# Weight preparation moved into the first stage of a four-layer graph kernel, and its first two stages put into one ordered region

## The chip, the cores and the metric

One core of a Trainium2 chip runs the whole program. Its engines work through their own instruction streams and wait for one another on semaphores: TensorE (PE, with its weight loads shown apart as PEld), VectorE (DVE), ScalarE (ACT), GpSimd (POOL) and SyncE (SP), which here does nothing but issue DMAs. The metric is device time in microseconds (us), the median of three runs: 2710.17 us before the change (2709.83 to 2714.95).

## The reference, cut to what matters

The input is 128 graphs of 128 nodes with 128 features each, and a 0/1 adjacency matrix per graph. Four attention layers follow one another, each as `x = x + layer(relu(layernorm(x)), adj, weights)`. Only layer 0 bears on the change:

```python
def layer0(x, A):                                  # x: 128 graphs x 128 nodes x 128
    D = abs(x[:, :, None, :] - x[:, None, :, :])   # every pair of nodes
    h = einsum('bijc,oc->bijo', D, W1) + b1        # 64 outputs for a pair
    m, v = mean and variance of h over all graphs and all pairs
    h = leaky((h - m) / sqrt(v + EPS) * g1 + be1)
    s = einsum('bijo,uo->biju', h, W2)[..., 0] + b2[0]
    A = softmax(where(A > 0, s, NEG))
    y = einsum('bij,bjc->bic', A, x) @ Wg.T + bg
    y = leaky(batchnorm(y)) ; return concat([x, y]) @ Wt.T + bt
```

The mean and the variance `m`, `v` are taken over all pairs of all graphs, so no score of any graph can be finished before every pair has been seen. The weights of layers 1 to 3 (`L1_...`, `L2_...`, `L3_...`) are only brought into another form at the start of the program: transposed, multiplied with one another, summed.

## The kernel before, in words

The program has four parts, one after the other in time.

**Preparation** (lines 185 to 369). Small weights are loaded as columns by DMAs issued on POOL (`column`, L201 and L203, and L220 to L223). Larger ones are loaded by SP (`raw`, L261) and ACT (L277 to L344). Then PE, ACT and DVE transpose and combine them: `transposed` (L263, L264), the columns `fw` of layer 1 (L276 to L288), `w2g` (L316 to L319), `of_f1`, `of_f2` and `parts_m` (L293 to L308), `aT` and `aq` (L330 to L340), `vpw` (L346), `pb_row` and `pb_bc` (L351 to L360), `q_avg` (L364 to L369). Their scratch tiles lie in the pool `wload`, which is closed before the first stage opens its own pools in the same memory.

**First stage**, `statistics` (L490). It sees every pair of nodes and collects mean and variance. `nodes(g)` handles 4 graphs: it loads `xg` (L525), takes means and variances of the rows on DVE (L530, L531), `rs` on ACT (L535, L536), `xn` on POOL (L539, L540), stores it to DRAM, transposes on PE (L545), takes the ReLU `he` on ACT (L548), stores that to DRAM too, and works out three bf16 parts `us` of `pu` (L557 to L566). `block(b, q)` takes 32 rows of a graph against the 64 (or 63) nodes after each: the differences `d` on DVE (L605) or on POOL (L610), their absolute value on ACT (L614) unless a maximum was taken, the product with `w1T` on PE into a PSUM tile `ph` (L631), and the sums of it on DVE (`bn_stats`, L643) or on ACT (L637). There are 512 blocks. Blocks which take the maximum need `both` (L512 to L516) and `w1T2` (L518), which are made from the identity and from `w1T`. Nine `d` and three `ph` are in rotation. After the last block a chain of some thirty small instructions (L657 to L700) makes `h_sc` and `h_bi` from the collected sums.

**Second stage**, `edge_attention` (L702). It begins with its constants: `off` and `at` on POOL (L716, L721), `in_half`, `in_other`, `not_own`, `upto`, `down_d`, `ones`, `least`, `room` and others on DVE (L728 to L758), and `own_d`, which needs `h_bi` (L768 to L776). Then `group(g)` handles 4 graphs: three loads on SP (L793 to L795), `adjb` on POOL (L802), `half` and `other` on POOL (L810, L811), `rank` and `key_row` on PE (L815 to L817), `more`, `ranks`, `pos` and `row` on DVE (L820 to L832), `in_row` on PE (L836), the selection matrices `inc` on DVE (L843). Beside it `parts` splits `xn` into three bf16 tiles (ACT L867, DVE L869, POOL L875 and L876), `values` makes `pz` and `zg`, `check` makes `pc` (L892 to L898), `bases` makes `base` and `edge` (ACT L908, POOL L910 and L912). `graph` then takes, for each graph, the differences of the nodes that are joined by an edge (`diff`, PE L923), their absolute value (ACT L930), the product with `w1T` (PE L934), `z` with `h_sc` and `h_bi` (ACT L937), and the scores; `attention` takes the softmax. Three groups can hold input tiles at a time (`B_IN`).

**Third stage.** The remaining layers, four graphs at a time. Which of two versions runs is read from the tile `types` at L2386, and the engines all stop there for it.

**What sets the order.** Inside each of the first two stages the order of instructions on PE, ACT, DVE and POOL is written out by a planner, `in_order` (L64). Each piece of work is a generator which says `yield engine, planned us, tiles taken, tiles freed` ahead of the instructions it emits. The planner keeps a time for each engine at which it is free and always takes the piece which can begin first; between pieces that can begin at the same time it takes the older. `yield "after", event` holds a piece until an event, `yield "wait", us` adds to its planned time. The planned times decide only the order; on the chip an engine goes through that order and waits where an input is late. Outside the two `manual_schedule` regions (L652 and L1091), the framework orders the instructions by itself. The two regions and what lies between them run one after the other: the pools of the second stage reuse the memory of the first.

## Time and profile before

One execution was profiled. Its own device time is 2713.54 us; its span from the first to the last instruction is 2711.7 us, so 1.8 us lie around the span. The profiled run is 3.4 us above the median of the three runs. The granted TensorE clock is 0.966 of full speed on average.

| stretch of the profiled execution | from | to |
|---|---|---|
| preparation, up to the first `xg` load | 0 | 21.5 us |
| first `nodes`, up to the first difference block | 21.5 | 35.6 us |
| difference blocks, to the last one of POOL | 35.6 | 1079.9 us |
| last block on PE | | 1090.0 us |
| second stage, up to its first full `diff` | 1090.2 | 1115.9 us |
| second stage, to the read of `types` | | 1772.4 us |
| third stage | 1772.4 | 2711.7 us |

| engine | busy in the span | share |
|---|---|---|
| PE | 2497.3 us | 92% |
| DVE | 2416.1 us | 89% |
| ACT | 2161.6 us | 80% |
| POOL | 1644.8 us | 61% |

How to read it: busy shares over the whole span mix stages with different limits, so the stages are looked at one by one. In a view of stretches each row gives, behind the stretch and its length, the busy time of every engine (and its instructions), then the granted clock of TensorE, the share of the DMA engines that was busy, and GB/s. In a timeline each row is a start time, a duration, the engine, the line of the program, the operation, what is written and read, and in brackets how long the engine had stood idle and what released it. `SPq` is an issue of a DMA on SyncE.

### The profile page before, as it was taken

To read this page: it belongs to the slowest core of one execution; us is meant where nothing else is said; L and a number is where in the kernel's file an instruction comes from. 1 tells how busy PE (TensorE), PEld (TensorE's weight loads), DVE (VectorE), ACT (ScalarE), POOL (GpSimd) and SP (SyncE) were. 2 spreads that over 40 slices of the span, in tenths; PEclk is the share of its full clock that TensorE was granted. 3 is DMA by queue.
4 is the path that set the end of the run, shared out by engine and by line. 5 is a ranking of instruction groups with operands and counts; after the bars stand their busy time and mean duration, and the time that the engine had idled before them with its cause. 6 is when DMAs were issued, how large, how long until landed. Compare 5 with 4: busy or idle time off the path is not lost. (4 is left out here: it accounts for less than half of the span.)

```text
span 2711.7 us, 51703 instructions
## 1 busy us (share of the span) xinstructions
PE 2497.3 (92%) x19597; PEld 1559.2 (57%) x19597; DVE 2416.1 (89%) x4660; ACT 2161.6 (80%) x3531; POOL 1644.8 (61%) x943
## 2 busy tenths in 40 slices
PE   6999999999999999799999999968988888898888
PEld 3334333434333333577777777756766767667666
DVE  6999999999999998788988888778988888889886
ACT  4999999999999999466566666568787877787885
POOL 7999999999999999635435343022333333333234
PEclk8999999999999999899999999979999999999999
DMA  2000000000000000523222231040211111111001
GB/s 69 16 27 30 24 24 28 24 24 24 24 24 24 24 20 9 161 74 100 81 85 86 78 100 42 17 137 6 62 29 54 36 44 44 41 42 33 9 2 33
DMA packets 134257, 122.62 MB, mean 45 GB/s; under 512 B 9504, under 2 KB 100960, under 8 KB 134000
## 3 DMA queue, kind: packets, MB, share of 16 engines
q1 hardware_dynamic: 131360, 117.83, 14.1%
q8 instruction: 158, 2.59, 0.4%
q10 hardware_dynamic: 2032, 1.31, 0.2%
q14 instruction: 99, 0.81, 0.1%
q0 software_dynamic: 608, 0.07, 0.0%
HBM read 73.05 MB, written 46.14 MB: 44 GB/s over the span
## 5 line engine op out<-in xcount | busy, mean ns | idle before, releaser
L610 POOL TENSOR_TENSOR d<-he 128x2016 f32<-128x2016 f32 (+1 forms) x272 | 959.8, 3559 | 15.0 <-DVE six L643 7.8
L631 PE MATMUL ph<-d,w1T 128*64 128x504 f32 (+1 forms) x4096 | 910.0, 594 | 22.9 <-DVE six L643 13.2
L614 ACT ACTIVATE d<-d 128x2048 f32<-128x2048 f32 (+1 forms) x448 | 832.2, 1888 | 18.1 <-POOL d L610 12.4
L631 PEld LDWEIGHTS ph<-d,w1T 128*64 128x64 f32 x4096 | 320.2, 136 | 545.0 <-issue 459.9
L605 DVE SCALAR_TENSOR_TENSOR d<-pt,he 128x2048 f32<-128x2048 f32 x240 | 541.4, 2269 | 0.7 <-PE ph L631 0.7
L643 DVE BATCH_NORM_STATS2 six<-ph 128x6 f32<-128x512 f32 (+1 forms) x704 | 435.8, 676 | 13.4 <-PE ph L631 12.0
L1568 POOL TENSOR_TENSOR xn<-xo,mv 128x512 f32<-128x512 f32 x64 | 73.9, 1155 | 324.8 <-DVE mv L1561 257.5
L975 PE MATMUL pl<-its,it 128*128 128x128 f32 x1280 | 168.2, 280 | 1.5 <-DVE its L968 1.2
L875 POOL CAST h<-xn 128x512 bf16<-128x512 f32 x32 | 21.5, 672 | 243.5 <-DVE xn L869 229.4
L637 ACT ACTIVATE ph<-ph 128x1008 f32<-128x1008 f32 x160 | 159.7, 998 | 9.8 <-PE ph L631 8.8
L975 PEld LDWEIGHTS pl<-its,it 128*128 128x128 f32 x1280 | 154.4, 193 | 15.0 <-DVE its L968 6.5
L1671 DVE SCALAR_TENSOR_TENSOR p<-z,mask 128x1024 f32<-128x1024 f32 x124 | 147.7, 1210 | 8.3 <-ACT z L1669 8.0
L1569 POOL TENSOR_TENSOR xn<-xn,rs 128x512 f32<-128x512 f32 x96 | 111.1, 1158 | 49.6 <-ACT rs L1565 37.9
L937 ACT ACTIVATE z<-ph,h_bi,h_sc 128x320 f32<-128x320 f32 x128 | 78.5, 617 | 74.5 <-PE ph L934 73.8
L923 PE MATMUL diff<-inc,h 128*128 128x320 bf16 x768 | 130.0, 306 | 2.9 <-DVE inc L843 2.5
L1669 ACT ACTIVATE z<-z 128x1024 f32<-128x1024 f32 x128 | 129.0, 1008 | 4.0
L930 ACT ACTIVATE d<-diff 128x640 f32<-128x640 f32 x128 | 89.8, 702 | 52.9 <-PE diff L923 51.7
L843 DVE SCALAR_TENSOR_TENSOR inc<-in_row,row 128x4 bf16<-128x4 f32 (+12 forms) x512 | 125.5, 315 | 1.2 <-PE in_row L836 1.2
L965 ACT CAST it<-pi 128x640 f32<-128x640 bf16 x128 | 87.0, 689 | 47.3 <-PE pi L962 46.1
L1568 POOL TENSOR_TENSOR xn<-x,mv 128x512 f32<-128x512 f32 x32 | 36.5, 1139 | 138.3 <-DVE mv L1561 65.9
L968 DVE TENSOR_TENSOR its<-pi,s 128x640 f32<-128x640 bf16 x128 | 102.9, 810 | 15.0 <-ACT it L965 14.1
L1700 PE MATMUL va<-p,vals 128*32 128x128 f32 x2048 | 107.8, 283 | 8.0 <-DVE vals L1685 7.8
(349 smaller groups left out, 5349.8 us busy)
## 6 DMA issues: line engine op xcount, KB each, us to landing
ht<-h SPq DMA_DIRECT2D x64, 256.0 KB, 2.8
xg<-in_x SPq DMA_DIRECT2D x32, 256.0 KB, 2.7
n<-ln_xn SPq DMA_DIRECT2D x32, 256.0 KB, 2.4
h<-he SPq DMA_DIRECT2D x32, 256.0 KB, 2.6
adj<-in_adj SPq DMA_DIRECT2D x32, 256.0 KB, 3.1
xn<-n SPq DMA_DIRECT2D x32, 256.0 KB, 2.7
xb<-in_x SPq DMA_DIRECT2D x32, 256.0 KB, 3.3
xb<-xb SPq DMA_DIRECT2D x32, 256.0 KB, 2.0
```

The costliest lines, as they stand in the source:

```text
L605: nc.vector.scalar_tensor_tensor(dv, own, 0.0, later, ALU.max, ALU.max if is_larger else ALU.subtract)
L610: nc.gpsimd.tensor_tensor(dv, later, own, ALU.subtract)
L614: nc.scalar.activation(d[:, 0 : 4 * n], d[:, 0 : 4 * n], AF.Abs, accum_out=sums[:, g, k : k + 1] if on_act else None,)
L631: nc.tensor.matmul(ph[64 * a : 64 * a + 64, t, 0:n], wt, x_, start=part == 0, stop=not is_larger or part == 3,)
L637: nc.scalar.activation(ph[:, :, 0:n], ph[:, :, 0:n], AF.Square, accum_out=squares[:, g, k : k + 1])
L643: nc.vector.bn_stats(six[g][:, 2 * by_bn.index((i, q)) + t, :], ph[:, t, 0:n])
L843: nc.vector.scalar_tensor_tensor(inc[:, :, e : e + n], in_row[:, :, 0:n], float(k + 1), row[:, :, 0:n], ALU.is_equal, ALU.subtract,)
L923: nc.tensor.matmul(diff[:, a, 0 : SLOT_N // 2], h[:, i, :], inc[:, a * SLOT_N // 2 : (a + 1) * SLOT_N // 2], start=m == 0, stop=m == 2,)
L975: nc.tensor.matmul(made["pl"][:, i, :], it[:, k, :], its[:, k, :], start=k == 0, stop=k == 4)
L1569: nc.gpsimd.tensor_tensor(xn, xn, bcast(rs, 2, P), ALU.mult)
L1669: nc.scalar.activation(z, z, AF.Exp, scale=1.0 - SLOPE)
L1671: nc.vector.scalar_tensor_tensor(p, z, 1.0, bcast(mask[:, i, :], 1, NH), ALU.max, ALU.mult)
```

## The change

The diff does the following.

- `x` for the first eight graphs (`raw_x`) is loaded at once, on SP, as the first and third DMA of the program; the weights come after it. The columns that POOL loaded are now loaded by SP; five square weights are loaded by ACT, after the activation table, which is now loaded at the start; all other weights are loaded by SP. The scratch tiles lie in pools on the other side of the memory, apart from those of the stages.
- The computing part of the preparation becomes generators of the planner (`first_weight`, `own_and_later`, `attention_weights`, `square_weights`), run under `others` as second piece of the first stage. So do the constants of the second stage (`edge_constants`). `both` is added up on POOL instead of DVE. The PSUM tiles of the preparation are taken from the stage's `ph`. One more piece may be under way (`A_UNDER_WAY + 1`).
- Both stages lie in one `manual_schedule` region. The planner returns the times at which each engine and PSUM bank becomes free, and the second stage is planned from those. The tiles that a group needs ahead of `inc` lie in the pool `mid`, outside the first stage's memory; pieces that use reused memory wait for the event `begun`, pieces that need the mean and variance wait for `stats`. The chain of small instructions that makes `h_sc` and `h_bi` is a generator (`total`) in a fixed order, with two of its products on PE joined into one.

```diff
-def in_order(makers, most, room, kept):
+def in_order(makers, most, room, kept, begun=None):
...
-    free_at = dict.fromkeys(AFTER, 0.0)
-    slots = {kind: [0.0] * n for kind, n in room.items()}
-    chains, events = [], {}
+    free_at = dict.fromkeys(AFTER, 0.0) if begun is None else dict(begun)
+    slots = {kind: [0.0] * n if isinstance(n, int) else list(n) for kind, n in room.items()}
+    chains, events = [], {"begun": max(free_at.values())}
...
+    nc.scalar.preload_act_table_set("natural_log_exp_and_others")
...
+    raw_x = [wl.tile([P, GB, P], F32, tag=f"x{g}", name=f"x{g}") for g in range(2)]
+    nc.sync.dma_start(raw_x[0], x_t[:, 0:GB, :])
...
+    raw("w1", w["L0_gnn_W1"], nc.sync)
+    nc.sync.dma_start(raw_x[1], x_t[:, GB : 2 * GB, :])
+    raw("wg", w["L0_gnn_Wg"], nc.scalar)
...
-        nc.gpsimd.dma_start(t[0:n], src)
+        nc.sync.dma_start(t[0:n], src)
...
+    def attention_weights():
+        yield "wait", 20.0
+        yield DVE, 2.9, "", ""
         nc.vector.memset(fw, 0.0)
...
+    def square_weights(psum2):
+        yield "wait", 8.0
+        yield PE, 1.3, "ph", ""
+        pt = psum2("w_ps").rearrange("p a (b c) -> p (a b) c", c=P)
+        for k, name in enumerate(("wg", "wt0", "wt1", "kw", "pw")):
+            nc.tensor.transpose(pt[:, k, :], raws[name], ident)
+        yield ACT, 0.9, "", "ph"
+        nc.scalar.copy(w_T, pt[:, 0:4, :])
...
+        yield "wait", 12.0
+        yield PE, 1.7, "ph", ""
+        pv = psum2("vw_ps")
...
+    def edge_constants():
+        yield "wait", 30.0
+        yield POOL, 0.6, "", ""
+        nc.gpsimd.iota(
+            off, pattern=[[1, P]], base=0, channel_multiplier=-1,
+            allow_small_or_imprecise_dtypes=True,
+        )
...
-            nc.vector.tensor_tensor(
-                both.rearrange("p (i j) -> p i j", j=64),
-                shifted(ident[:, 1:65], QR), bcast(ident[:, 0:QR], 2, 64), ALU.add,
-            )
...
+            def own_and_later():
+                yield POOL, 3.9, "", ""
+                nc.gpsimd.tensor_tensor(
+                    both.rearrange("p (i j) -> p i j", j=64),
+                    shifted(ident[:, 1:65], QR), bcast(ident[:, 0:QR], 2, 64), ALU.add,
+                )
+                yield DVE, 0.68, "", ""
+                nc.vector.tensor_scalar(both, both, -1.0, None, ALU.mult)
+                yield "done", "both"
...
+            def first_weight():
+                yield "wait", 4.0
+                yield PE, 0.3, "ph", ""
...
+                if g < len(raw_x):
+                    xg = raw_x[g]
+                    yield "wait", 4.0 + 1.2 * g
+                else:
...
+            makers = [partial(nodes, 0), others]
...
+            begun = dict.fromkeys(AFTER, 1.0) | {POOL: 1.5, ACT: 5.0, DMA: 22.0}
+            free_at, slots = in_order(
+                makers, A_UNDER_WAY + 1, {"d": A_D, "ph": 3} | two, A_KEPT, begun
+            )
+        wl_pool.__exit__(None, None, None)
...
+        def total(psum, done):
+            yield "after", "begun"
+            yield DVE, 1.0, "", ""
...
+            yield PE, 0.4, "", ""
+            nc.tensor.matmul(pm[:, 1:4], q_avg, bn_m, start=True, stop=True)
+            yield DVE, 3.6, "", "p"
...
+            yield "done", "stats"
...
-            off = one_of("off", [P, P])
-            nc.gpsimd.iota(
...
-                xn, ht = tile_f("xn", B_IN), tile_f("ht", B_IN)
+                xn, ht = tile_i("xn", F32), tile_i("ht", F32)
...
+                yield "after", "begun"
                 for a, b in ((0, 2), (2, 4), (4, len(SLOTS))):
                     work = sum(0.1 + 0.00104 * GB * n for n in SLOTS[a:b])
                     yield DVE, work, "", "p" if b == len(SLOTS) else ""
+                    if a == 0:
+                        inc = b3p.tile([P, GB, SLOT_N], BF16, tag="inc", name="inc")
...
+                yield "after", "stats"
                 yield ACT, 0.53, "", "p"
                 z = made["z"][:, i, :]
                 nc.scalar.activation(z, ph, AF.Identity, bias=h_bi, scale=h_sc)
...
-            with tc.manual_schedule(engines=ORDERED):
-                in_order(
...
+            in_order(
+                makers, B_GROUPS, {"p": banks[0:6], "q": banks[6:7], "in": B_IN, "w": B_W, "d": 3, "it": 3, "ge": 1, "eT": 2, "yt": 2, "xb": 2}, {"p": 1}, free_at
+            )
...
-    statistics()
-    edge_attention()
+    with tc.manual_schedule(engines=ORDERED):
+        edge_attention(*statistics())
```

## The prediction

> **What bounds the kernel now.** I read the page's slices first (POOL, DVE and PE are full in the first stage, PE and DVE in the second), then the timeline at the start and at the border between the stages, then busy time by stretch. The chain of waits stops at the read of `types`, so it says nothing of these stages. From the timeline of the start:
>
> ```profile
> 0.74 0.59 SPq L261 DMA_DIRECT2D raw<-in_L_gnn_W  x1
> ...
> 20.70 0.76 PE L359 MATMUL ppb<-pb_row,ones_row 1*128 1x128 f32 x2 [0.71 <-DVE pb_row L357]
> 21.49 6.49 SPq L525 DMA_DIRECT2D xg<-in_x  x3
> ...
> 24.25 0.29 DVE L530 BATCH_NORM_STATS2 ln_s<-xg 128x6 f32<-128x128 f32 x1
> ...
> 35.58 17.60 POOL L610 TENSOR_TENSOR d<-he 128x2016 f32<-128x2016 f32 x5
> ```
>
> `x` is asked for only when the last product of the preparation is out of the scratch memory; its first use follows 2.76 us later, the first difference block 11.3 us after that. From the timeline of the border, the last rows of the first stage and the first of the second:
>
> ```profile
> 1089.48 0.60 PE L631 MATMUL ph<-d,w1T 128*64 128x504 f32 x2
> ...
> 1090.17 0.39 SPq L793 DMA_DIRECT2D adj<-in_adj  x1
> ...
> 1093.35 0.61 POOL L802 CAST adjb<-adj 128x512 bf16<-128x512 int32 x1 [13.46 <-DMA adj<-in_adj]
> ...
> 1106.20 0.39 PE L815 MATMUL rank<-upto,other 128*128 128x128 bf16 x4
> ...
> 1115.94 1.49 PE L923 MATMUL diff<-inc,h 128*128 128x320 bf16 x5 [2.47 <-DVE inc L843]
> ```
>
> POOL stands idle from 1079.9, 13.46 us long; the loads start when PE has finished; the first stream of edge differences comes 25.9 us after PE's end (1115.94 - 1090.08). Busy time by stretch (columns: PE, PEld, DVE, ACT, POOL, granted clock, DMA share, GB/s):
>
> ```profile
> 0.00:21.86 21.86, 8.77 (x32) 4.70 (x32) 7.67 (x40) 3.87 (x10) 11.48 (x27) 0.95 0.32 80
> 35.50:45.00 9.50, 6.58 (x26) 2.37 (x28) 8.05 (x7) 6.13 (x6) 9.50 (x4) 0.57 0.25 81
> 45.00:1079.90 1034.90, 1015.10 (x5156) 406.93 (x5154) 1020.00 (x1259) 1013.97 (x1062) 1017.30 (x358) 1.00 0.07 23
> 1090.00:1150.00 60.00, 42.73 (x319) 31.15 (x318) 47.49 (x173) 27.70 (x54) 45.90 (x44) 0.83 0.60 182
> 1150.00:1772.00 622.00, 593.41 (x5171) 461.21 (x5169) 520.89 (x1348) 382.24 (x813) 239.31 (x216) 0.98 0.23 73
> ```
>
> The first stage is full on four engines at once: 98.6% DVE, 98.3% POOL, 98.1% PE, 98.0% ACT. The second is PE's: 95.4%. So the time lies in three places: before the blocks, the blocks, the border.
>
> **Start.** The load of `x` goes from 21.49 to about 0.74, SP's first slot (the row of the W1 load). It shares the DMA engines with weights; of the old loads at the start the slowest took 4.7 us to land, the lone `xg` loads in 2.7. I take 3.0, so the first statistics stand at 3.7. The table load (1.28 us, now ahead of ACT's loads) ends long before ACT's first use. From first statistics to first block 11.3 us stay: 15.0 instead of 35.6, **20.6 us gained**. What could be late inside those 11.3: the sum of `both` moves from DVE (2.29 us) to POOL. The trace has this pair of engines on nearly one shape: differences take 3.56 us on POOL, 2.27 on DVE, factor 1.57, so 3.6 us, from 1.6 to about 5.2, just before POOL is wanted at 5.3. The Trainium skill, "GPSIMD Engine Reference" (4.1 Engine selection), puts two-input work at about twice VectorE's time: 4.6 us, end 6.2, and the start later by 0.9. I keep the row.
>
> SP now issues some 26 further loads, 0.4 to 0.6 us each: the last at about 15, landed by 20; the generators are planned for 21 and later. Behind them on SP is the first store of `xn`; a third `nodes` needs its tile, but is planned after DMA's 22.0.
>
> A second weighing, the clock. "TensorE: Matmul & The Clock Gate" (Part 1, "What's actually happening") says that half rate is the default and is lifted by about 3.4 us of sustained work; by it the new first `nodes` runs cold, like the old one, whose eight `pu` products took 1.76 us against 1.1 warm (33.1 us over 30 groups in the blocks). The trace grants 1.00 at the start and falls to 0.50 only after PE's pause behind 21.5. By the row, one set of `nodes` saves 0.45 in transposes (1.11 against 0.66) and 0.66 in `pu`, 1.1 us. I leave it out and use it for the range.
>
> **Blocks.** Moved in: DVE 7.67 - 0.3 (memsets that stay first) = 7.3 us of preparation, and 3.4 of constants (busy 3.45 of 3.6 us from 1095.6), together 10.7; PE 8.8; ACT 3.87 - 1.28 = 2.6; POOL two iotas of 0.24. The old cover was an otherwise idle machine; now they lie in a stage whose DVE has 14.9 us free in 1034.9. The waits of DVE there are 8.8 us on PE's `ph`, which are not slots that work may fill at will: PE waits as long for DVE (13.2 in the page's row), in turn, with three `ph`. Lower end: all of it fits, 0. Upper: DVE's 10.7 and PE's 8.8 never overlap, 19.5. Nearest row: at the ramp (35.5 to 45) DVE has 1.45 us idle. 10.7 - 1.4 = **9.3 us lost**. PE's part is taken beside it, since PE waited for DVE anyway.
>
> **Border.** The planner starts the second stage from the times at which each engine is free, so its work on PE still comes behind PE's last block, but POOL's behind POOL's last at 1079.9 and the loads earlier still. For three groups POOL has `adjb` 0.61 and `other`, `half` 1.15 each: 8.7 us, inside the 10 us in which PE and ACT finish. Then `rank` follows PE's last block instead of coming 16.1 us later (1106.20 - 1090.08). From `rank` to the stream of `diff` it took 9.7 us; in that stretch DVE must now also do the chain of small sums, which the old order laid largely beside the last blocks (1081.9 to 1095.4): about 28 instructions of 0.15 us, 4 us. So 25.9 becomes 13.7: **12.2 us gained**. Next late is DVE (sums, `row`, `inc` in one queue), then `z`, which waits for `h_bi`; behind it on ACT are the other groups' copies.
>
> Ends: none of it, and 4 us lost, if the loads or tiles come no earlier and the sums stand in one row; or all that PE lost there, 17.3 us idle between 1090 and 1150 and a clock of 0.83 over 42.7 busy us, some 7: 24 us. If PE, fed with `pz` and `rank` at once, keeps its clock, part of the 7 comes back. 12 is the middle of these, and the one that the rows give.
>
> The second stage after it is kept at 622 us of PE-bound work, the third unchanged.
>
> **Sum.** -20.6 + 9.3 - 12.2 = -23.5: span 2711.7 to 2688.2, the profiled execution 2713.54 to 2690.0. The median of the runs was 2710.17, 3.4 below it, so I forecast **2686.7**.
>
> **Rivals.**
> 1. *Border gain fails*: `inc`, `base` and `zg` wait for `begun` anyhow, and DVE is the queue for both chains. For it: from 1091.3 to 1119.6 DVE is busy 20.7 of 28.3. Against it: POOL, busy 21.6 there, begins 13 us earlier. -20.6 + 9.3 + 0 = -11.3: 2698.9.
> 2. *Work vanishes in gaps*: DVE's 14.9 free us take the weights, PE stays warm. For it: four engines that wait for each other by turns leave slack on all. Against: no wait on DVE exceeds 1.3 us. -20.6 + 2 - 18 = -36.6: 2673.6.
> 3. *The added load costs twice*: 19.5 in the blocks and nothing at the border: -1.1, 2709, no change. For it: the weights hold one of three `ph` across engines. Against: four holdings only.
> 4. *Slower*: the second stage's order is planned anew from uneven starting times and banks, and PE's share there falls. Its place is 1150 to 1772, where PE is busy 593.4 us. It decides when it eats 23.5 + 5.4 us: 622 + 29 = 651, a share of 91.2% instead of 95.4. At 90% the stage takes 659, +37: 2724. For it: the planner's durations are estimates. Against: the same pieces, the same number of tiles in rotation.
> That the change does not do what it says (the loads stay behind a wait on SP) is the first rival at the border; at the start nothing stands ahead of `x`.
>
> **How the numbers follow.** Forecast with its own spread (2679 to 2694): 0.62. Rival 1: 0.14. Rival 2: 0.12. Rival 3: 0.06. Rival 4: 0.06. A measurement of this kernel can tell about 0.2%, 5.4 us, from no change. Faster: 0.62 + 0.14 + 0.12 = 0.88; within: 0.06; slower: 0.06. The range takes in rival 1 and most of rival 2: 2672 to 2702.
>
> **What would show it.** First statistics near 3.7 and first `d` near 15; the last POOL block 11 us earlier than 1079.9; POOL not idle after it, `adjb` at once; `diff` within 15 us of PE's last block; the read of `types` near 1749. Wrong if DVE shows waits on weight loads in the first 25 us, if the blocks stretch by far more or less than 9 us, if SP still issues the `adj` loads only after the last block, or if PE's share in the second stage moves by over one point.

## The result, and the profile after

The changed kernel takes 2702.51 us (2699.1 to 2704.5 in seven runs) against 2711.97 us (2709.62 to 2721.8) for the kernel before in the same comparison: ratio 0.996, 95% interval 0.9945 to 0.9974. It is faster, as forecast, but by 9.5 us (0.35%) and not by 23.5; 2702.5 lies just outside the forecast's range of 2672 to 2702. The profiled execution took 2704.5 us with a span of 2702.7, 9.0 below the 2711.7 of before, and I work with that pair.

In the changed kernel the stage's lines moved: `d` is L706 on POOL and L701 on DVE, `ph` L727, the block statistics L739, `nodes` L618 to L662, `rank` L887, `inc` L917, `diff` L1001. From the timeline of the changed kernel, the start and then the border between the stages:

```profile
3.98 0.29 DVE L623 BATCH_NORM_STATS2 ln_s<-x 128x6 f32<-128x128 f32 x1 [2.91 <-DMA x<-in_x]
...
12.71 3.55 POOL L706 TENSOR_TENSOR d<-he 128x2016 f32<-128x2016 f32 x1
...
24.41 0.73 SPq L865 DMA_DIRECT2D adj<-in_adj  x1
...
1087.33 15.67 PE L727 MATMUL ph<-d,w1T 128*64 128x512 f32 x72
1090.63 1.74 POOL L874 CAST adjb<-adj 128x512 bf16<-128x512 int32 x3
...
1104.26 0.38 PE L887 MATMUL rank<-upto,other 128*128 128x128 bf16 x4 [1.26 <-ACT ph L733]
...
1124.67 1.49 PE L1001 MATMUL diff<-inc,h 128*128 128x320 bf16 x5 [2.40 <-DVE inc L917]
```

The first block starts at 12.7 instead of 35.6. The graph loads are issued at 24.4, a thousand microseconds ahead of their use; POOL goes on with `adjb` as soon as its last block ends at 1090.6, and `rank` follows PE's last block (1103.0) by 1.3 us. These moves did what they say. But the last block is late, not early, and the full stream of `diff` comes 21.7 us after it. Busy time by stretch of the changed kernel (columns as before: PE, PEld, DVE, ACT, POOL, granted clock, DMA share, GB/s):

```profile
12.50:46.00 33.50, 23.00 (x90) 9.30 (x89) 31.14 (x28) 14.32 (x17) 32.71 (x12) 0.80 0.53 151
46.00:76.00 30.00, 24.13 (x100) 8.89 (x100) 27.18 (x84) 20.04 (x21) 0.77 (x2) 0.89 0.00 1
76.00:1090.60 1014.60, 990.75 (x5016) 396.84 (x5016) 998.17 (x1232) 986.30 (x1034) 996.78 (x353) 0.99 0.08 24
1103.00:1125.00 22.00, 9.20 (x70) 6.79 (x71) 17.07 (x64) 8.06 (x17) 9.60 (x10) 0.73 0.51 155
1125.00:1763.00 638.00, 616.78 (x5405) 482.76 (x5413) 557.20 (x1415) 399.71 (x849) 260.98 (x240) 0.98 0.25 77
```

The hole is in the first two rows. In the first 34 us of the blocks DVE is busy for 31.1 and PE only for 23.0; in the next 30 us POOL works for 0.77. Over the same 63.5 us from its own first block the kernel before had PE busy 59.6 us, here 47.1. From 76 us on the stage is full again (PE 97.6%, before 98.1%).

| step, from the profiled executions | before | after | measured | forecast |
|---|---|---|---|---|
| start of the program to first block | 35.6 | 12.7 | -22.9 | -20.6 |
| first block to PE's last | 1054.5 | 1090.3 | +35.8 | +9.3 |
| PE's last block to the stream of `diff` | 25.9 | 21.7 | -4.2 | -12.2 |
| stream of `diff` to the read of `types` | 656.5 | 637.9 | -18.6 | 0 |
| third stage | 939.3 | 940.1 | +0.8 | 0 |
| sum | | | -9.1 | -23.5 |

(The read of `types` is taken here, and in the table below, at the instruction that writes `types`, 0.1 to 0.2 us ahead of the read.) So the start was right, the loss in the blocks was nearly four times the forecast, and the second stage, which I had set to zero, paid half of it back. By these rows, without that unforeseen gain the changed kernel would have been slower than before. What does DVE do in those 34 us? The timeline of DVE in the changed kernel (start, duration, line):

```profile
20.55 3.02 DVE L326 TENSOR_TENSOR prod<-w1c,a1b 128x256 f32<-128x256 f32 x1
23.60 0.42 DVE L328 TENSOR_REDUCE wsums<-prod 128x8 f32<-128x256 f32 x1
...
26.92 0.41 DVE L326 TENSOR_TENSOR prod<-w1c,a1b 128x256 f32<-128x256 f32 x1
...
27.82 2.95 DVE L329 COPY fw<-wsums 128x24 f32<-128x24 f32 x1
...
33.27 0.27 DVE L386 TENSOR_TENSOR pb_row<-pb_row,vw_ps 1x128 f32<-1x128 f32 x1
33.56 1.15 DVE L387 TENSOR_SCALAR pb_row<-pb_row 1x128 f32<-1x128 f32 x1
...
38.96 2.94 DVE L340 COPY w2g<-gw 128x2 f32<-128x2 f32 x1
...
42.72 3.53 DVE L340 COPY w2g<-gw 128x2 f32<-128x2 f32 x1
```

and POOL's for the same time:

```profile
26.93 3.81 POOL L706 TENSOR_TENSOR d<-he 128x2016 f32<-128x2016 f32 x1
...
31.09 10.79 POOL L706 TENSOR_TENSOR d<-he 128x2016 f32<-128x2016 f32 x3
42.67 3.55 POOL L706 TENSOR_TENSOR d<-he 128x2016 f32<-128x2016 f32 x1 [0.79 <-PE ph L727]
75.45 1.04 POOL L632 TENSOR_TENSOR ln_xn<-xg,ln_mv 128x512 f32<-128x512 f32 x1 [29.23 <-DVE ln_mv L624]
```

A copy of 24 numbers per partition lasts 2.95 us; in the preparation of before the two such copies lasted 0.17 and 0.24. It ends at 30.77, and POOL's block ends at 30.74. The copy of two numbers that starts at 38.96 ends at 41.90, the run of three POOL blocks at 41.88; the one of 42.72 ends at 46.25, POOL's block at 46.22. The second product, 0.41 us, started 0.01 us ahead of POOL's block of 26.93: here it is the block that is longer, 3.81 instead of 3.55. Two more blocks of this stage, at 23.24 and 38.15, last 3.73, and both begin while a DVE product is still under way; before the change none of the 272 blocks was lengthened so. So whichever comes second waits for the other. No list of waits shows it, since the time is counted as busy. Reductions (0.42), memsets and L386, which has one operand in PSUM (0.27), are not touched. Added up over the seven weight rows of over a microsecond, each against its short form, this is 16.3 us of DVE between 20.5 and 46 us. The last row of POOL shows what follows: the statistics of the third group stand behind all that on DVE, and POOL waits 29.23 us for them.

### The profile page after: what moved, and what is told of

Its sections match the earlier page's. It is cut to its first block, busy times and chain, and to the rows that moved or that the text cites. A ratio compares the mean times of both kernels' runs of the same rounds, so it can differ in the third digit from the quotient of the medians.

```text
span 2702.7 us, 51582 instructions
## 1 busy us (share of the span) xinstructions
PE 2498.0 (92%) x19584; PEld 1558.9 (58%) x19595; DVE 2437.8 (90%) x4648; ACT 2160.7 (80%) x3527; POOL 1632.8 (60%) x923
## 4 chain that ended last, share of the span: by engine, by line
PE 45%; DVE 30%; ACT 14%; issue 6%; POOL 2%; DMA 1%; SPq 0%; ACTq 0%; DVEq 0%; POOLq 0%
PE ph L727 13%; DVE d L701 6%; ACT d L710 6%; DVE six L739 5%; PE pl L1056 4%; PE diff L1001 4%; DVE p L1752 3%; PE ph L1014 2%; PE sp L1024 2%; PE po L1709 2%; ACT ph L733 2%; PE va L1781 1%; DVE s L1640 1%; PE ph L1911 1%; PE sm L1781 1%
## 5 line engine op out<-in xcount | busy, mean ns | idle before, releaser
L706 POOL TENSOR_TENSOR d<-he 128x2016 f32<-128x2016 f32 (+1 forms) x272 | 960.7, 3564 | 14.3 <-PE ph L727 8.8
L727 PE MATMUL ph<-d,w1T 128*64 128x512 f32 (+1 forms) x4096 | 919.8, 599 | 37.7 <-DVE six L739 25.0
L727 PEld LDWEIGHTS ph<-d,w1T 128*64 128x64 f32 x4096 | 320.7, 137 | 566.8 <-issue 489.1
L701 DVE SCALAR_TENSOR_TENSOR d<-pt,he 128x2048 f32<-128x2048 f32 x240 | 541.5, 2270 | 1.4 <-PE ph L727 1.4
L739 DVE BATCH_NORM_STATS2 six<-ph 128x6 f32<-128x512 f32 (+1 forms) x704 | 436.1, 676 | 16.3 <-PE ph L727 15.1
L988 POOL TENSOR_TENSOR base<-base,own_d 128x512 f32<-128x512 f32 x32 | 42.7, 1334 | 179.8 <-PE ph L1014 124.0
L1001 PE MATMUL diff<-inc,h 128*128 128x320 bf16 x768 | 128.8, 304 | 3.9 <-DVE inc L917 3.9
L917 DVE SCALAR_TENSOR_TENSOR inc<-in_row,row 128x8 bf16<-128x8 f32 (+12 forms) x512 | 126.5, 315 | 0.8 <-PE in_row L908 0.8
L1649 POOL TENSOR_TENSOR xn<-x,mv 128x512 f32<-128x512 f32 x32 | 36.1, 1129 | 136.8 <-DVE mv L1642 73.7
L1997 POOL TENSOR_TENSOR xh<-xh,xo 128x512 f32<-128x512 f32 x32 | 46.9, 1467 | 106.6 <-DVE xh L1718 82.8
```

The source lines that it names most:

```text
L701: nc.vector.scalar_tensor_tensor(dv, own, 0.0, later, ALU.max, ALU.max if is_larger else ALU.subtract)
L706: nc.gpsimd.tensor_tensor(dv, later, own, ALU.subtract)
L727: nc.tensor.matmul(ph[64 * a : 64 * a + 64, t, 0:n], wt, x_, start=part == 0, stop=not is_larger or part == 3,)
L739: nc.vector.bn_stats(six[g][:, 2 * by_bn.index((i, q)) + t, :], ph[:, t, 0:n])
L917: nc.vector.scalar_tensor_tensor(inc[:, :, e : e + n], in_row[:, :, 0:n], float(k + 1), row[:, :, 0:n], ALU.is_equal, ALU.subtract,)
L1001: nc.tensor.matmul(diff[:, a, 0 : SLOT_N // 2], h[:, i, :], inc[:, a * SLOT_N // 2 : (a + 1) * SLOT_N // 2], start=m == 0, stop=m == 2,)
```

## Experiments

Every kernel below was timed once, beside one run of the kernel before; only e3_late was timed again (e14_late5). The seven runs of the changed kernel lie within 5.4 us, so totals that differ by less than that are not told apart. All times in the table are us of the profiled execution; the first column is the start of POOL's first block, the others the start of PE's last block, `h_bi`, the first instruction of `diff` (its full stream comes up to 3.2 us later), the read of `types`, and the span.

| kernel | first block | last `ph` | `h_bi` | `diff` | `types` | span |
|---|---|---|---|---|---|---|
| before | 35.6 | 1089.5 | 1095.2 | 1113.0 | 1772.3 | 2711.7 |
| after | 12.7 | 1102.4 | 1119.2 | 1121.8 | 1762.6 | 2702.7 |
| e1_copies | 36.1 | 1133.6 | 1139.3 | 1157.4 | 1812.6 | 2752.3 |
| e2_memsets | 36.6 | 1098.9 | 1104.6 | 1122.7 | 1778.2 | 2718.2 |
| e3_late | 12.7 | 1081.6 | 1098.6 | 1101.2 | 1740.8 | 2676.9 |
| e4_fresh | 12.9 | 1102.4 | 1114.9 | 1126.1 | 1779.5 | 2719.5 |
| e5_direct | 12.7 | 1102.0 | 1118.8 | 1121.4 | 1760.0 | 2700.3 |
| e6_group0 | 12.8 | 1102.2 | 1119.8 | 1120.7 | 1787.3 | 2729.6 |
| e7_both | 12.8 | 1080.5 | 1098.3 | 1099.3 | 1766.0 | 2705.1 |
| e8_edge | 12.7 | 1091.0 | 1107.8 | 1110.4 | 1749.0 | 2689.5 |
| e9_sets | 12.8 | 1094.6 | 1111.4 | 1114.0 | 1754.8 | 2694.8 |
| e10_bias | 12.8 | 1080.8 | 1095.0 | 1102.9 | 1745.9 | 2688.7 |
| e11_act | 12.7 | 1096.2 | 1110.4 | 1118.4 | 1762.6 | 2702.4 |
| e12_sets_edge | 12.8 | 1072.9 | 1089.5 | 1092.0 | 1733.0 | 2673.9 |
| e13_both_late | 12.8 | 1090.9 | 1111.5 | 1112.5 | 1767.6 | 2703.1 |

My theory: small DVE instructions beside POOL's blocks wait for the block, and that stretched the first stage. The rival: the amount of work moved to the ramp did it, whatever its kind.

### The price of one small copy: e1_copies and e2_memsets

Both are the kernel before with 24 extra DVE instructions spread over the first stage, one kind each. Both kinds are planned at 0.2 us, so the rest of the order is the same in both:

```diff
...
+            def tiny():
+                yield "wait", 200.0
+                for _ in range(24):
+                    yield DVE, 0.2, "", ""
+                    nc.vector.tensor_copy(tiny_b, tiny_a)
+                    yield "wait", 25.0
...
-            makers = [partial(nodes, 0)]
+            makers = [partial(nodes, 0), tiny]
...
-                in_order(makers, A_UNDER_WAY, {"d": A_D, "ph": 3} | two, A_KEPT)
+                in_order(makers, A_UNDER_WAY + 1, {"d": A_D, "ph": 3} | two, A_KEPT)
```

In e2_memsets the copy is `nc.vector.memset(tiny_b, 0.0)`.

> The kernel before, with 24 copies of 128x24 fp32 from SBUF to SBUF on VectorE added in the first stage, one every 25 us from 200 us on; nobody waits for their result. Theory P (such an instruction cannot run beside a GpSimd instruction and waits for the end of it): a copy is recorded at 1 to 3.5 us instead of about 0.2, and the last GpSimd block comes 25 to 60 us after 1079.9. Theory Q (only the amount of work on VectorE counts): 24 x 0.2, at most 6 us later, copies at 0.2.

> The same with 24 memsets of the same tile in place of the copies, planned at the same 0.2 us. Theory P: [...]0.1 us each and the stage ends within 4 us of before. Theory Q: the same as the copies, up to 6 us later.

e1_copies took 2754.24 us, e2_memsets 2720.08. The groups of DVE instructions, by line (count, then busy time and mean ns of one), of e1_copies:

```profile
L654 DVE COPY tiny_b<-tiny_a 128x24 f32<-128x24 f32 x24 | 44.1, 1836 | 0.0
```

and of e2_memsets:

```profile
L654 DVE MEMSET tiny_b<- 128x24 f32 x24 | 1.9, 78 | 0.0
```

The same size in the same places: 1.836 us against 0.078. The shortest of the copies took 0.444, the longest 3.205, just under one block of POOL (3.56). One of them, with the POOL block beside it:

```profile
221.03 3.56 POOL L610 TENSOR_TENSOR d<-he 128x2016 f32<-128x2016 f32 x1
223.08 1.54 DVE L654 COPY tiny_b<-tiny_a 128x24 f32<-128x24 f32 x1
```

The block ends at 224.59, the copy at 224.62. All 24 copies end so in the trace, 0.03 to 0.04 us after the POOL instruction that was running when they began (23 difference blocks and one product of `ln_xn`); all 24 memsets begin and end inside a POOL instruction. This is the wait itself, and no rival is left for it. The difference in total is 34.2 us, 1.42 us for a copy: 81% of the 42.2 us by which DVE was held reaches the end.

The copies did what theory P expected: POOL's last block came 42.0 us later. The memsets came out short, as P said, but POOL's last block ended 7.2 us later and not within 4, and the kernel took 10 us more than the 2710.1 of the run of before beside it. I put that to the order, which the extra piece changes, but did not test it.

### The weights moved to the end: e3_late, and again as e14_late5

```diff
     def attention_weights():
-        yield "wait", 20.0
+        yield "wait", 1060.0
```

> The changed kernel with attention_weights planned at 1060 us, the end of the first stage, where GpSimd has done its last block, instead of 20 us. Theory P: its copies (fw, w2g) fall from 2.9 to 3.5 us to under 0.4; the constants of the second stage, which lasted 0.2 to 0.3 us while GpSimd stood idle for 29 us, now meet a busy GpSimd and some of them last 1 to 3 us; the first stage's last GpSimd block comes 0 to 15 us earlier than 1090.6. Theory Q (too much at once in the ramp, whatever it is): durations as they were, the 29 us of GpSimd shrink to under 10, and the stage ends 15 to 25 us earlier.

2678.65 us: 24 less than the changed kernel. PE's last block starts 20.8 us earlier, and POOL's last block ends 24.4 us earlier. That is more than theory P had allowed for (0 to 15) and lies in the range of theory Q (15 to 25): this run alone doesn't tell the two apart, since moving the work takes both its waits and its amount from the ramp. The durations speak for P: at the end of the stage the same copies took 0.55 to 1.13 us, and the first product 2.77. It is also the best version with all weights in place, so it was timed again, in four runs beside seven of the kernel before.

> The kernel of e3_late again, timed in five rounds against the kernel before. Theory P (waits for GpSimd's blocks, taken from the ramp): 2677 to 2681, ratio to before 0.987 to 0.990. Rival (its 2678.65 was one lucky run): nearer to the changed kernel's 2702.5, ratio above 0.993.

2680.23 us (2677.7 to 2683.7) against 2713.57; ratio 0.9882, interval 0.9866 to 0.9899. Over three times the changed kernel's gain (33.3 us against 9.5), for one number.

### The four copies alone: e5_direct

```diff
-            nc.vector.tensor_reduce(sums.rearrange("p s h -> p (s h)"), prod, AX.X, ALU.add)
-            nc.vector.tensor_copy(
...
-            )
+            for k in range(3):
+                e = 3 * HH * m + HH * k
+                nc.vector.tensor_reduce(
+                    fw[:, :, e : e + HH], prod.rearrange("p (s h) d -> p s h d", h=HH), AX.X, ALU.add
+                )
...
-            nc.vector.tensor_reduce(gw, prod2, AX.X, ALU.add)
-            nc.vector.tensor_copy(w2g[:, :, P + s], gw)
+            nc.vector.tensor_reduce(w2g[:, :, P + s], prod2, AX.X, ALU.add)
```

> The changed kernel, its weights in the same place of the order, but the four small copies that lasted 2.95 to 3.5 us in the ramp are gone: the sums are reduced straight into fw (three reduces instead of one reduce and one copy) and into w2g. VectorE's work as planned stays the same within 1 us. Theory P (waiting for GpSimd is what the moved work costs): VectorE is free about 10 us earlier in the ramp, the last GpSimd block comes 7 to 14 us before 1090.6. Theory Q (too many instructions at once in the ramp, whichever): within 3 us of 1090.6.

2702.13 us, nothing gained, though the four slow copies are gone, and POOL's last block ends at 1090.2. That is what theory Q forecast (within 3 us of 1090.6); P's 7 to 14 us did not come. DVE's timeline in e5_direct shows why:

```profile
24.60 2.67 DVE L326 TENSOR_TENSOR prod<-w1c,a1b 128x256 f32<-128x256 f32 x1
...
31.16 3.48 DVE L384 TENSOR_SCALAR pb_row<-pb_row 1x128 f32<-1x128 f32 x1
...
38.95 3.33 DVE L336 TENSOR_TENSOR prod<-w2g,a2b 128x256 f32<-128x256 f32 x1
42.31 0.42 DVE L337 TENSOR_REDUCE w2g<-prod 128x2 f32<-128x256 f32 x1
42.65 3.29 DVE L395 COPY aT<-araw 128x256 f32<-128x256 f32 x1
```

In the changed kernel the second L326 took 0.41 and the step of `pb_row` 1.15; now they, and a copy of `aT`, wait. While POOL's blocks stand one behind another, the next instruction of the same kind takes the wait over. Taking out these four was worth nothing. The total alone tells against the theory as I had stated it, with a fixed price for each copy; the rows show that the waits were still there, on other instructions.

### Memsets in place of the weights: e9_sets and e12_sets_edge

This pair bears most on the rival. The weights' work stays at the ramp, in amount and place, but as instructions that e2 showed not to wait:

```diff
-            nc.vector.tensor_tensor(prod, w1c, a1b[:, :, m * DH : (m + 1) * DH], ALU.mult)
...
+            for k in range(3):
+                nc.vector.memset(prod, 0.5)
+            nc.vector.memset(fw[:, :, 3 * HH * m : 3 * HH * (m + 1)], 0.01)
...
     def edge_constants():
-        yield "wait", 30.0
+        yield "wait", 1050.0
```

The second of these edits, the edge constants, is in e12_sets_edge only.

> The changed kernel with the weights' own DVE instructions in the ramp (products, reductions and copies of attention_weights, the copies of aT, the last step of pb_row) replaced by memsets of about the same count and of at least the same unlocked length (three memsets of 128x256 for each product with its reduction, 0.8 us). Places in the order and all waits of the planner stay. Left out: the values of fw, w2g, of_f1, of_f2, parts_m, a1bc, q_avg, aT and pb_row, which become constants, so the outputs are not the reference's; the edge constants stay. Theory P (the waits for GpSimd's blocks stretch the first stage, not the amount of DVE work): none of these memsets lasts over 0.6 us, POOL no longer stands idle for 29 us, and POOL's last block ends at 1066 to 1080 instead of 1090.6; the edge constants, which then meet a busy POOL, give back 3 to 8 us of it; total 2680 to 2693. Rival A (7 us of extra DVE work at the ramp, whatever its kind, break the pipeline's start): POOL's last block stays at 1087 to 1091, total 2699 to 2703.

> e9_sets with the edge constants planned at 1050 us instead of 30, so that of the moved DVE work only memsets stand at the ramp, with their full 7 us. Left out: the same values as in e9_sets. Theory P (port waits stretch the stage): no DVE instruction of these lines waits at the ramp, POOL has no idle time over 3 us before 90 us, and its last block ends at 1066 to 1073; what the edge constants wait at the end costs 0 to 5 us of that. Rival A (7 us of DVE work of any kind at the ramp break the start): POOL idles over 15 us again before 90 us, and its last block ends at 1078 to 1083.

e9_sets took 2696.61 us, between the two expectations: POOL's last block ended at 1082.8, and POOL still stood idle for 22.8 us from 45.0 on. No memset waited, but the edge constants, which in the changed kernel met an idle POOL, met a busy one, and three in a row waited. DVE's timeline in e9_sets:

```profile
20.73 1.05 DVE L327 MEMSET prod<- 128x256 f32 x3
...
35.89 2.07 DVE L413 TENSOR_SCALAR tmp<-off 128x128 f32<-128x128 f32 x1
37.99 3.54 DVE L414 SCALAR_TENSOR_TENSOR tmp<-off,tmp 128x128 f32<-128x128 f32 x1
41.57 3.53 DVE L415 SCALAR_TENSOR_TENSOR in_half<-off,tmp 128x128 bf16<-128x128 f32 x1
```

With these taken from the ramp as well, e12_sets_edge took 2675.74 us. POOL's last block ended at 1057.8, earlier than either theory had said. Its stretches:

```profile
12.50:46.00 33.50, 28.93 (x138) 13.04 (x139) 29.03 (x62) 23.01 (x26) 33.50 (x11) 1.00 0.53 151
46.00:76.00 30.00, 28.79 (x150) 10.76 (x148) 28.45 (x39) 26.42 (x29) 22.82 (x10) 1.00 0.14 45
```

PE is busy 57.7 us of the 63.5, near the 59.6 of before, and POOL's longest idle time there is 4.9 us instead of 29.2 (I had expected none over 3). From first block to PE's last it takes 1060.7 us, 6.2 more than before, where the changed kernel took 35.8 more. So the weights' 7 us of DVE work, left at the ramp as memsets, do not break the start: their amount is not the cause. About 30 us of the stretch go with the two edits together. Which share belongs to which is not shown, since e12 also took the edge constants, 3.4 us of work and the waits in it, from the ramp. That 7 us fit there but all 10.7 would not, whatever their kind, is not excluded by this pair; the three waits of e9 and the pair e1 and e2 speak against it.

### Other ways around the wait: e8_edge, e11_act, e13_both_late

e8_edge joins e3 and e5 and plans the edge constants at 6 us instead of 30; e11_act is e10_bias with the four copies of `aT` on ACT (`nc.scalar.copy`); e13_both_late is e3 with the edge constants at 1050.

> e3 with e5's reduces, and the constants of the second stage, which need no load, planned at 6 us, where VectorE stands idle before the first difference block, instead of 30. Theory P: few waits there, since GpSimd runs only instructions of 1 us, and the ramp loses its other 4 us of work and the one wait of 3.6 us: the last block 4 to 9 us before e3's 1066.2. Theory Q: the same direction, 4 to 5 us. If the constants delay the first block instead, the start moves from 12.7 to over 15 us and nothing is gained.

> e10_bias, with the four copies of aT on ACT instead of DVE. Theory P: in e3_late one of these copies waited up to 2.94 us on DVE; ACT has no such wait with POOL, so POOL's last block ends 1 to 4 us earlier than in e10_bias. Rival (the edge constants behind them take the wait over, or ACT, as full as DVE, pays it): within 1 us of e10_bias.

> e3_late with the edge constants also planned at 1050 us instead of 30. Theory P: the waits of e3_late at the ramp (a copy of aT 2.94 us and L429 3.58 us) go or shrink to one; the edge constants at the end meet the last blocks of POOL, with one or two waits of up to 3.6 us, so POOL's last block ends at 1062 to 1068 (1066.2 in e3_late), total 2673 to 2681. Rival: they are late for the second stage's first rank, and its first diff comes later than 19.6 us after PE's last block, total 2682 or more.

2691.38, 2704.27 and 2704.98 us: all three lose against e3_late, and each theory-P forecast missed (POOL's last block at 1077.2, 1079.0 and 1073.0). DVE's timelines show each time that the wait found another instruction. In e8_edge:

```profile
16.25 3.58 DVE L444 TENSOR_SCALAR ident<-ident 128x128 bf16<-128x128 f32 x1
19.75 3.53 DVE L446 TENSOR_SCALAR least<-at 128x16 f32<-128x16 f32 x1
```

These stand ahead of `us`, and PE's first block starts at 27.4 instead of 18.1. In e11_act the copies of `aT` took 0.64 to 0.66 us each on ACT, beside POOL's blocks, so ACT did not wait for them; but three edge constants waited 3.67, 3.46 and 3.54 us on DVE from 38.3 on. In e13_both_late copies of `aT` waited 3.00 and 2.54 us at the ramp, and at 1066 and 1069 a copy to `fw` 3.17 and a product 3.84 (0.57 to 1.13 and 0.41 to 2.77 in e3). There the rival came true as well: the first `rank` stood 1.47 us behind `upto`, one of the late edge constants, `diff` came 21.6 us after the start of PE's last block (19.7 in e3), and the second stage was longer too (next section but one). Which instruction meets POOL's block could not be told from the planned times in any of the three.

### The border: e10_bias

```diff
             def with_bias(g):
-                yield "after", "begun"
+                yield "after", "stats"
```

on top of e3_late (the diff shows this second edit alone). In the changed kernel the chain of sums took 15 us, from 1104.24 to `h_bi` at 1119.25. Two of its rows, with POOL's beside them, from the timeline of the changed kernel:

```profile
1108.20 1.16 POOL L951 TENSOR_TENSOR h<-xn,h 128x512 bf16<-128x512 f32 x1
1108.36 1.01 DVE L782 TENSOR_TENSOR act_mm<-act_m 128x1 f32<-128x1 f32 x1
...
1109.31 1.26 POOL L934 TENSOR_TENSOR xb<-xb,bt_bc 128x512 f32<-128x512 f32 x1
1109.40 1.19 DVE L784 SCALAR_TENSOR_TENSOR bn_m<-act_v,act_mm 128x1 f32<-128x1 f32 x1
```

Each product of one number per partition ends with the POOL instruction beside it: 1109.37 and 1109.36, 1110.59 and 1110.57.

> e3_late with one line more: with_bias waits for the event stats instead of begun, so the three additions of 1.26 us on POOL that lay beside the chain of small sums come after it. Theory P at the border (single-element additions on DVE wait for the whole of POOL's instruction): two of the three waits of 1.0 to 1.2 us in the chain vanish; h_bi is ready 14 to 15.5 us after PE's last block instead of 17.0, the first diff 1.5 to 3 us earlier, total 2674 to 2678 against 2678.65. Rival (the chain is held by the other groups' DVE work and PE's product, in their order): h_bi within 1 us of 17.0 after PE's last block, total within 1.5 us of 2678.65.

The three rows in question, from the timeline of e10_bias:

```profile
1087.01 0.16 DVE L782 TENSOR_TENSOR act_mm<-act_m 128x1 f32<-128x1 f32 x1
1087.21 0.16 DVE L784 SCALAR_TENSOR_TENSOR bn_m<-act_v,act_mm 128x1 f32<-128x1 f32 x1
...
1094.52 0.16 DVE L511 TENSOR_TENSOR h_sc<-af_rs,g 128x1 f32<-128x1 f32 x1 [0.67 <-POOL af_rs L510]
```

0.16 instead of about 1.1, and `h_bi` comes 14.2 us after the start of PE's last block instead of 17.1, as expected. The time did not follow: `diff` came 22.1 us after that start instead of 19.7, and the total is 2690.62, not 2674 to 2678. PE's rows show why. From the timeline of e3_late:

```profile
1101.24 0.42 PE L1001 MATMUL diff<-inc,h 128*128 128x320 bf16 x1 [1.54 <-DVE inc L917]
```

and of e10_bias:

```profile
1102.55 0.58 PE L908 MATMUL in_row<-row,ranks 128*128 128x128 bf16 x4 [6.53 <-DVE row L904]
1102.93 1.80 PE L1001 MATMUL diff<-inc,h 128*128 128x320 bf16 x6
```

In e3_late, as in the changed kernel, `diff` waits for `inc`, and DVE begins `inc` right behind the chain, 16.8 us after PE's last block ended. In e10_bias it begins 13.9 us after it. But the one line drew another order for PE: `in_row` of the next group now stands ahead of `diff`, and PE waits 6.53 us for that group's `row`. The full stream of `diff` follows at once, 21.5 us after PE's last block, against 21.9 in e3_late. So the chain does hold `diff` in the changed kernel; what a shorter chain is worth by itself stays unmeasured, since the new order took the gain again. Of the 12 us to e3_late 5.1 are there at the read of `types`; the rest is in the third stage, whose length, with the same code, lies between 935.5 and 942.8 us in these runs.

### The order of the second stage: e4_fresh, e6_group0, e7_both

```diff
-                makers, B_GROUPS, {"p": banks[0:6], "q": banks[6:7], "in": B_IN, "w": B_W, "d": 3, "it": 3, "ge": 1, "eT": 2, "yt": 2, "xb": 2}, {"p": 1}, free_at
+                makers, B_GROUPS, {"p": 6, "q": 1, "in": B_IN, "w": B_W, "d": 3, "it": 3, "ge": 1, "eT": 2, "yt": 2, "xb": 2}, {"p": 1}
```

is e4_fresh, and e6_group0 is

```diff
-            makers = [partial(total, psum, own_d), *(partial(group, g) for g in range(n_parts))]
+            makers = [partial(group, 0), partial(total, psum, own_d), *(partial(group, g) for g in range(1, n_parts))]
```

e7_both is e3, e5 and e6 together.

> The changed kernel with the second stage planned from zero for all engines and banks, as before, instead of from the times at which the first stage frees them. If the uneven starting times made the better order of the second stage, PE's idle time from the first stream of edge differences to the read of types goes from 21 back to about 31 us, and the read of types comes about 10 us later than 1762.7. If the order got better for another reason (tiles that are ready early, the places of the waits), it stays within 3 us.

> The changed kernel with the first group ahead of the chain of small sums (total) in the planner's list, nothing else. If the sums standing ahead of ranks, row and inc in VectorE's queue are what ate the gain at the border, the first stream of edge differences comes 4 to 9 us earlier than 21.7 us after PE's last block, and z waits for h_bi instead; if the two chains cost VectorE the same in either order, within 2 us.

> e5, e6 and the late weights of e3 together. If the three costs are separate: the stage ends as in e3 or up to 3 us earlier, the border is as short as in e6, total 2665 to 2677; if the border's gain is lost again later, 2677 to 2682.

2721.28, 2731.42 and 2706.94 us. The first stage and the first `diff` of e4 and e6 are within 4.3 us of the changed kernel's; what moves is the length from `diff` to `types`. In e4 PE's idle time there goes back to 30.0 us, as forecast, and the read of `types` comes 17 us later, not 10. In e6 the full stream of `diff` comes 18.9 us after PE's last block instead of 21.7, between the two forecasts. e7 keeps that border (19.2 us) but misses its 2665 to 2682 by the second stage. From the table: before 659.3, e4 (planned from zero) 653.4, after 640.8, e6 666.6, e7 666.7. The middle of that stage in stretches, of the changed kernel:

```profile
1200.00:1700.00 500.00, 494.58 (x4400) 388.45 (x4407) 449.60 (x1138) 324.50 (x687) 217.76 (x201) 0.99 0.26 82
```

and of e6_group0:

```profile
1200.00:1700.00 500.00, 483.97 (x4280) 378.31 (x4286) 429.76 (x1099) 317.03 (x679) 218.40 (x202) 1.00 0.26 82
```

98.9% of PE against 96.8% at nearly the same clock and with the same code, only in another order. So, against before, this stage varied with its planned order from -21 (e5, 638.6) to +7 us (e7), and no edit at its first microseconds can be priced without it. The good order is not a property of planning from the true starting times: e13_both_late, e6 and e7 are planned that way too and take 655.1 to 666.7. So I take the gain in the changed kernel for a property of the list that came out, not of the idea; no run isolates what in the list makes it.

## Why the prediction was wrong, point by point

**Start, -20.6 forecast, -22.9 measured: right.** First statistics at 3.98 (forecast 3.7). The sum of `both` on POOL took 3.60 us, as taken from the row of the differences and not the 4.6 that a factor of two would have made. The 2.3 us beyond the forecast come from a step that fell away: before, POOL normalised a third group (33.05 to 35.58) ahead of the first block. In the second weighing I misread the row: the first `pt` took 1.11 us and eight `pu` products 1.80, as cold as before (1.11 and 1.76). The trace's first clock record lies at 16.4 us before the change and at 21.0 after it; the 1.00 that a view prints ahead of it is not measured. It made no difference, since I had left the 1.1 us out.

**Blocks, "10.7 - 1.4 = 9.3 us lost", 35.8 measured: this step failed.** I priced DVE's moved instructions at their durations in the preparation, where POOL issued loads and streamed no blocks, and only asked whether DVE had room. Beside POOL's blocks the same instructions last up to 3.5 us. Even the upper end (19.5) assumed unchanged durations. The blocks of before could not show the wait, since they pair POOL with statistics and with differences that read one operand from PSUM (2.27 us, unchanged). But the border of the same trace did show it:

```profile
1100.65 1.47 POOL L876 TENSOR_TENSOR h<-xn,h 128x512 bf16<-128x512 f32 x1
1101.03 1.17 DVE L776 TENSOR_SCALAR own_d<-ident,own_c 128x128 f32<-128x128 f32 x1
```

The same `own_d` takes 0.29 us in the changed kernel, where it meets no POOL instruction at its start; here it ends 0.08 us behind POOL's addition. The Trainium skill, "SBUF — State Buffer" (Who interferes with whom), states the rule: DVE and GpSimd share a pair of ports, which is taken as an exclusive lock. A copy or a scalar operation in a mode that uses both ports holds it for the whole instruction, whoever issues first, and a DVE instruction with two inputs in SBUF contends with a GpSimd instruction that reads SBUF. The ends that coincide, the block of 3.81 us, the unaffected memsets and the PSUM operand agree with it. By that page each of the 21 copies, scalar operations and two-input operations among the moved weights was to be priced at up to POOL's 3.56 us: an upper end of 75 us, an estimate, instead of 19.5. Seven of them waited, 16.3 us in all, and the blocks took 26.5 us more than forecast. How much of the 26.5 these waits made is not measured by itself.

The smaller part of the step was wrong the other way. With the waits at the ramp gone (e12) the blocks stretch by 6.2 us, and PE's busy time there rises by 6.9 (1038.75 against 1031.88) while its idle time stays (22.0 against 22.7). So DVE's moved work, for which I had charged 9.3 us, left no idle time on PE, and what remains is about the size of PE's moved work (8.8), which I had laid beside it for free. In the changed kernel PE's idle time is 40.2 us and its busy time 1050.1: half of the stretch is PE waiting, half is longer PE time, of which 8.8 us was moved in. The trace grants half the clock for 30.7 us of this stretch, in which PE is busy 21.9 us, against 8.2 and 5.3 us before; if such work takes 1.6 to 2 times as long (eight cold `pu` products took 1.80 us, warm ones 1.1), that is 6 to 8 us more, an estimate, and most of the rest.

**Border, -12.2 forecast, -4.2 measured: mis-sized.** POOL, the loads and `rank` came as said. The term "about 28 instructions of 0.15 us, 4 us" was the error: the chain took 15.0 us, of which three single-element instructions waited 3 us for POOL, about 3.5 us are other groups' DVE work in between, and PE's first product of it came only at 1107.85, behind `rank`, `pz` and `pc`. `inc` stands behind the chain on DVE, at 1119.58, though its input `in_row` was ready at 1114.9, and `diff` waits for `inc`. What a shorter chain would give is not measured: in e10, where it was 3 us shorter, another order on PE held `diff`.

**Second stage, 0 forecast, -18.6 measured: left out.** PE's busy time there fell from 625.6 to 617.1 us, for a reason that I did not find (at the border it fell too, from 10.5 to 8.9), and its idle time from 30.9 to 20.8. The fourth rival had the mechanism, an order planned anew from uneven starting times, with the opposite sign. e4 shows that the starting times alone make 12.6 us of difference. But e6, e7 and e13, which keep them, lose the gain: the runs show no rule for its sign, and that it came out as a gain was luck.

**The rivals.** The first came nearest in time (2698.9 against 2702.5), and in part in cause: DVE was the queue for both chains at the border, and two thirds of the gain there were lost. But it kept 9.3 us for the blocks and 0 for the second stage, so its nearness is luck: 26.5 us more were lost in the one and 18.6 won in the other. The third (2709) had the blocks at 19.5 us for the amount of work, which is not what cost there. Of the signs that I named, the block stretch did speak ("by far more or less than 9 us"), and so did PE's share, which rose from 95.3% to 96.7%.

## What to carry to other kernels

Before moving DVE work under a stage in which GpSimd streams, sort it by operands. In these runs reductions, memsets and instructions with an operand in PSUM went in at their own length; copies, scalar operations and two-input operations in SBUF took up to a whole GpSimd instruction each, even at two numbers per partition, and when four of them were removed the wait moved to others. Put such work where GpSimd is idle or runs out of blocks; here one planned time (20 to 1060) was worth 22 us (2702.5 to 2680.2). And where a planner writes the order, an edit at a border also draws a new order for the stage behind it, which has to be measured by itself.

## What the runs showed of the hardware that was not expected

The wait of DVE for POOL is not shown as idle: it lengthens the instruction's own duration (a copy of 128x24 from 0.17 to between 0.44 and 3.2 us), so a DVE that looks full may be held. The ends give it away: those of all 24 copies of e1 fall on the ends of POOL's instructions within 0.04 us. And the wait goes both ways: POOL's block of 26.93 was 0.26 us longer behind a product of 0.41. ACT's copies in e11, 0.64 to 0.66 us each beside the same blocks, showed no such wait.
